# Cross-attention and quantised feed-forward on one core: a text group's last values added straight from PSUM, the x1 fill spread over the units, weight maxima run beside ScalarE's background

## The chip, the cores and the metric

One core of one Trainium2 chip runs the whole program. The time is device microseconds of that core, from the program's start to its end; several runs of a kernel give a median, and one further run is recorded by the hardware profiler. Engines are named as the profile names them: PE (TensorE, with PEld for its weight loads), DVE (VectorE), ACT (ScalarE), POOL (GpSimd) and SP (SyncE, which only issues DMAs here).

## The reference, cut to what matters

```python
# x (4, 1024, 512), ctx (4, 1024, 512); 16 heads of 32
q = layernorm(x) @ Wq + bq ; k = ctx @ Wk + bk ; v = ctx @ Wv + bv
# mask per batch: 768 image tokens attend within their own chunk of 256;
# 256 text tokens attend to all image tokens and causally to text
x1  = x + softmax(q k^T / sqrt(32) where mask) v @ Wo + bo
xq  = fake_quant(layernorm(x1))          # one scale: the maximum over the whole tensor
h   = fake_quant(silu(xq @ wg_q^T) * (xq @ wu_q^T))   # again one scale for all of it
out = x1 + h @ wd_q^T                    # wg_q, wu_q, wd_q: int8-rounded, a scale per row
```

The two scales over whole tensors cut the program into three stages that follow each other: attention up to x1, gate and up products, down product.

## The kernel before, in words

**Tiling of the attention.** The 4096 tokens are cut into 16 chunks of 256 (`B * NQB`); of the four chunks of a batch three are image and the last is text. A `Block` is one chunk of queries, and a group is four heads of it (four groups). An image group has one part, since it sees only its own chunk of keys; a text group has four parts, one for each chunk of keys (part 3 is the causal diagonal). A `Unit` is a block, a group and a part: 112 units in all, 12 image units and then 16 text units for each of the first three batches; the last batch runs one image block (4 units), the text block (16) and two image blocks (8).

**The loop.** `for n in range(len(units) + V_LAG)` (L821) works on three units at a time. Iteration n does, in this order: `weights` of unit n-5 (scores transposed into PSUM with the row maximum subtracted, L488 and L492 on PE, exponential on ACT, L494); `maxima` of unit n (scores L442 on PE, then on DVE four row maxima, L445 for image and L449 for text, with the mask added first, L448, where a text part is odd); the sums over keys of unit n-5 on POOL (L514); `minus_maxima` after a group's last part (POOL L465 and L466, and in the next iteration a transposing DMA, L473, whose tile `nmT` the `weights` of that group's part 0 read); the x1 fill (L848 to L855); a background item; `values` of unit n-6 (L532 on PE, 4 heads side by side); ACT's copy of the result (L881); one large step of projections or of the output product (`large`, all at L225 on PE); the second background item; and so on. The four engines PE, DVE, ACT and POOL run in exactly the order in which the code issues their work (`manual_schedule`, L777); SP's queue is not in that list, and its order is chosen when the program is built.

**PSUM.** All tiles of the attention stage come from one pool of 8 banks, each 128 x 512 f32. A bank is used again as soon as its readers are done. The bank `av` of `values` (L522) has two halves of 256 columns: half 0 takes the values (L532), half 1 takes the sums of the exponentials over the keys (L555, matmuls with a block of ones), which are made only for a group's last part.

**A text group's sum over its parts.** Part 0 is copied to `oT` by ACT (L543); parts 1 and 2 are added to `oT` by DVE straight from PSUM (L545). The last part is not added there: after the sums have come in, ACT copies both halves to SBUF (`avs`, L881), and in the next iteration `quotient` (L566) takes the reciprocal of the sums on DVE (L567), adds `oT` to the values in SBUF on DVE (L569, text only) and multiplies on POOL (L570).

**From unit 84 on** (`LATE`, L658) the large steps are halved, so that iterations are shorter there.

**x1 in DRAM.** x1 begins as the output bias (a DMA from SP, L853) plus x (an accumulating DMA that POOL issues, L855), chunk by chunk; later `Output.load` reads a chunk (L584), the output product is added (L588), moments are taken (L595 to L598), and POOL's queue writes it back (L601).

**The background.** A queue holds the layer norm's steps (`statistics` on DVE, `deviation` and `apply` on ACT and POOL), the moments of x1 (DVE) and, from iteration 49 on, the 22 tiles of the gate and up weights: `largest` (DVE L636 to L638), `quantise` (ACT L641, POOL L642), and a transposing DMA (L646). An iteration takes one item; if that was `quantise`, it takes the next one too.

**After the attention.** L1055 is the gate and up product, L1146 and L1158 the down product. The change does not touch them.

Of the kernel before, what the change touches and what calls it, by code (L numbers as in the profile page):

```python
# [14 lines left out]
ALU = mybir.AluOpType  # L15
# [5 lines left out]
B, N, C = 4, 1024, 512  # L21
# [5 lines left out]
NQB = N // QB  # L27
# [15 lines left out]
def kernel(ctx: ExitStack, tc: tile.TileContext, x, kv, Wq, bq, Wk, bk, Wv, bv, Wo, bo, clip_x, clip_down, w_gate, w_up, w_down, out):  # L43
    nc = tc.nc
# [77 lines left out]
    with ExitStack() as actx:  # L122
# [9 lines left out]
        def bank(name):  # L132
            return ps_b.tile([P, 512], F32, tag="b", name=name)
# [212 lines left out]
        background = deque()  # L346
# [54 lines left out]
        def rows_of(j):  # L401
            return slice(j * D, (j + 1) * D)
# [115 lines left out]
        def values(u):  # L518


            k, g = u.k, u.g
            av = bank(f"av_{u.n}").rearrange("p (a q) -> p a q", a=2)  # L522
            if u.part == 0 and g == 0:
                k.begin()
            o = k.oT[:, g, :]
            diag = k.text and u.part == TEXT
            last = u.part == u.parts - 1
            va = V[k.keys[u.part]]
            for n in range(2):
                cols = slice(P, QB) if diag and n else slice(0, QB)  # L530
                for j in range(4):
                    nc.tensor.matmul(  # L532
                        av[rows_of(j), 0, cols],
                        va[:, n, g * P + j * D : g * P + (j + 1) * D],
                        u.pT[:, j, n, cols],
                        start=(n == 0),
                        stop=(n == 1),
                        tile_position=(0, j * D),
                        skip_group_check=True,
                    )  # L540
            if not last:
                if u.part == 0:
                    nc.scalar.copy(o, av[:, 0, :])  # L543
                else:
                    nc.vector.tensor_tensor(o, av[:, 0, :], o, ALU.add)  # L545
            if last:
                terms = []
                if ("sum", k.n, g) in state:
                    terms.append((state.pop(("sum", k.n, g)), slice(0, QB)))
                if u.direct:  # L550
                    terms += [(u.pT[:, :, n, :], slice(P, QB) if diag and n else slice(0, QB)) for n in range(2)]
                for n, (sp, cols) in enumerate(terms):
                    for j in range(4):

                        nc.tensor.matmul(  # L555
                            av[rows_of(j), 1, cols],
                            ones[:, :D],
                            sp[:, j, cols],
                            start=False,
                            stop=(n == len(terms) - 1),  # L560
                            tile_position=(0, j * D),
                            skip_group_check=True,
                        )
                avs = small.tile([P, 2, QB], F32, tag="avs", name=f"avs_{u.n}", bufs=2)

                def quotient():  # L566
                    nc.vector.reciprocal(avs[:, 1, :], avs[:, 1, :])  # L567
                    if k.text:
                        nc.vector.tensor_tensor(avs[:, 0, :], avs[:, 0, :], o, ALU.add)  # L569
                    nc.gpsimd.tensor_tensor(o, avs[:, 0, :], avs[:, 1, :], ALU.mult)  # L570

                return avs, av, quotient

# [77 lines left out]
        units = []  # L651
        for b in range(B):
            for qb in range(NQB) if b < B - 1 else (0, TEXT, 1, 2):
                k = Block(b, qb)
# [68 lines left out]
        def need_rows(kind, c, g, n):  # L723

            while rows_done.get((kind, c), 0) <= g:
                advance(n)

        def need_values(c, n):
            while ("v", c) not in done:
                advance(n)  # L730
# [56 lines left out]
                nc.tensor.matmul(tail.pos[i], tail.k.oT[:, cc, i * P : (i + 1) * P], W["Wo"][:, cc, :], start=False, stop=(cc == NCC - 1))  # L787

        weight_stages, n_weights = deque(), 0
        last_small = None  # L790

        def send(a):
# [28 lines left out]
        for n in range(len(units) + V_LAG):  # L821
            previous = units[n - 1] if 0 < n <= len(units) else None
            if n < len(units):
                u = units[n]
                half = u.part % 2
                for c in u.k.keys[2 * half : 2 * half + 2] if u.k.text else u.k.keys:
                    need_rows("k", c, u.g, n)
                need_rows("q", u.k.c, u.g, n)

            def shifts_of_previous():  # L830
                if previous is not None and previous.part == previous.parts - 1:
                    shifts(previous)

            if T_LAG <= n < len(units) + T_LAG:
                sums = weights(units[n - T_LAG], shifts_of_previous)
            else:
                shifts_of_previous()
                sums = None
            if n < len(units):
                maxima(u)  # L840
            if sums is not None:
                sums()
            if n < len(units) and u.part == u.parts - 1:
                minus_maxima(u)
            if n in (2, 3, 4, 5):
                (spread, sigmoids, product, total)[n - 2]()

            for first, c in ((True, (n - 5) // 3), (False, (n - 7) // 3)):  # L848
                rows = slice(c * QB, (c + 1) * QB)
                if not 0 <= c < B * NQB or (n - (5 if first else 7)) % 3:  # L850
                    continue
                if first:
                    nc.sync.dma_start(x1_d[rows, :].rearrange("(t p) c -> p t c", p=P), bo_b.unsqueeze(1).to_broadcast([P, QB // P, C]))  # L853
                else:
                    nc.gpsimd.dma_start(x1_d[rows, :], x_tok[rows, :], accum_op=ALU.add, max_dma_last_dim=C)  # L855
            t = units[n - T_LAG] if T_LAG <= n < LATE else None
            crowded = t is not None and t.k.text and t.part > 1
            while sum(b.__name__ == "moments" for b in background) > 1:
                background.popleft()()
            f = background.popleft() if background and n > 0 and not (crowded and background[0].__name__ == "deviation") else None  # L860
            if f is not None and f.__name__ in ("deviation", "apply", "quantise"):
                f()
                f = background.popleft() if background and f.__name__ == "quantise" else None
            fs = list(later)
            later.clear()
            for g in fs:
                g()
            ends = None
            if n >= V_LAG:
                v = units[n - V_LAG]  # L870
                need_values(v.k.keys[v.part], n)
                if v.part == 0 and v.g == 0:
                    while len(outputs) + len(whole) >= OUTS:
                        step_output()
                if v is units[-5]:
                    tail.load()
                ends = values(v)
            if ends is not None:
                avs, av, quotient = ends
                if n < len(units) + V_LAG - 1:  # L880
                    nc.scalar.copy(avs, av)  # L881
            large(n)
            while whole:
                finished(whole.pop(0))
            if f is not None:
                f()
            if ends is not None and n < len(units) + V_LAG - 1:
                later.append(quotient)
            if n == len(units) + V_LAG - 2:
                assert not outputs  # L890
                tail_products(0, (0, 1))

            if weight_stages and quantised[0]:
                weight_stages.popleft()()
            if can_small(n):
                small_step()
            prepare_next(n)
            if n > n_img and n_weights < 2 * NIC and not weight_stages and len(background) < 2:
                stages = weight_unit(n_weights)
                background.extend(stages[:2])  # L900
                weight_stages.append(stages[2])
                n_weights += 1
            if n < LATE and spent + BIG < target(n) and can_big(n + 1):
                big_step()
            if n >= V_LAG:
                u = units[n - V_LAG]
                if u.part == u.parts - 1 and u.g == NCC - 1 and u is not units[-1]:
                    whole.append(u.k)
# [74 lines left out]
    with gctx:  # L983
# [83 lines left out]
        for tb in range(NTB):  # L1067
# [5 lines left out]
            for ic in range(NIC):  # L1073
                last = tb == NTB - 1 and ic >= NIC - 2
# [64 lines left out]
    for n, tb in enumerate(order):  # L1139
# [9 lines left out]
        o = out_tok[tb * TB : (tb + 1) * TB, :].rearrange("(t p) c -> p t c", p=P)  # L1149
# [65 lines left out]
```

## Time and profile before

| what | value |
|---|---|
| median of 3 runs | 1118.52 us (1116.16 to 1120.01) |
| the profiled execution's own time | 1117.18 us |
| its span in the profile | 1115.3 us |
| mean granted TensorE clock | 0.987 |
| busy: PE, DVE, POOL, ACT | 97%, 76%, 48%, 47% |
| attention | 0 to about 872 us |
| gate and up products | about 872 to 1032 us |
| down product | 1032 us to the end |
| text groups in the trace (iterations of their `values`) | about 180 to 287, 384 to 491, 588 to 690, 716 to 809 us |

"Busy" counts the time in which an engine has at least one instruction in work. An idle stretch of an engine is listed with what ended it. The granted clock is the share of TensorE's full clock that its throttle lets through. The chain of waits runs back from the last instruction, at each step to what released it. Times within the trace count from the span's start.

### The profile page before, as it was taken

What the parts mean: (1) busy time and instruction counts of PE and PEld (TensorE: products, weight loads), DVE (VectorE), ACT (ScalarE), POOL (GpSimd) and SP (SyncE); (2) the same over time, 40 slices, a digit from 0 to 9 for tenths busy, and PEclk for the clock granted to TensorE, in tenths of its full rate; (3) what the DMA queues carried; (4) which work ended last, traced back from release to release, by engine and by line L of the source; (5) the groups of instructions that cost most, each with busy time, mean ns of one, the idle gap of its engine ahead of it and who ended that gap; (6) DMA issues with size and microseconds to landing.
All of it is one profiled execution on the core that took longest, in us unless ns stands there. A gap on an engine that the chain in (4) does not pass through costs nothing.

```text
span 1115.3 us, 32159 instructions
## 1 busy us (share of the span) xinstructions
PE 1087.0 (97%) x13851; PEld 585.9 (53%) x13851; DVE 846.9 (76%) x1316; ACT 522.1 (47%) x941; POOL 531.0 (48%) x615
## 2 busy tenths in 40 slices
PE   9998999999999999999999999989999899998998
PEld 5555555465655555565545556655554344443444
DVE  2555678797688959778786887987777788877887
ACT  3344444354445435454533455554443565553653
POOL 1224447678764567775446666765642221110110
PEclk9998999999999999999999999998999899999999
DMA  7369636355645454332222122212211698311895
GB/s 236 93 202 284 144 80 133 72 117 102 121 63 115 94 117 85 108 82 65 92 73 67 42 77 61 60 53 80 72 66 58 203 287 247 75 34 39 300 382 193
DMA packets 138262, 135.91 MB, mean 122 GB/s; under 512 B 56060, under 2 KB 103432, under 8 KB 136712
## 3 DMA queue, kind: packets, MB, share of 16 engines
q1 hardware_dynamic: 115600, 91.91, 29.6%
q0 software_dynamic: 22208, 41.42, 14.1%
q8 instruction: 108, 1.77, 0.7%
q10 hardware_dynamic: 312, 0.53, 0.2%
q14 instruction: 34, 0.28, 0.1%
HBM read 79.96 MB, written 50.07 MB: 117 GB/s over the span
## 4 chain that ended last, share of the span: by engine, by line
PE 81%; DMA 6%; DVE 5%; POOL 3%; issue 2%; ACT 2%; SPq 1%; DVEq 0%; POOLq 0%; ACTq 0%
PE po L225 9%; PE av L532 8%; PE pv L225 8%; PE pp_q L225 8%; PE pp_kv L225 8%; PE s L442 8%; PE t L492 7%; PE pg L1055 7%; PE pu L1055 7%; PE t L488 3%; PE av L555 3%; PE pd L1158 2%; POOL sp L514 2%; DMA xt<-x_d 2%; ACT pT L494 1%
## 5 line engine op out<-in xcount | busy, mean ns | idle before, releaser
L494 ACT ACTIVATE pT<-t 128x512 f32<-128x512 f32 x448 | 231.3, 603 | 135.7 <-PE t L492 135.5
L514 POOL TENSOR_TENSOR sp<-pT 128x1024 f32<-128x1024 f32 x59 | 140.8, 2386 | 173.8 <-ACT pT L494 173.7
L514 POOL TENSOR_TENSOR sp<-sp,pT 128x1024 f32<-128x1024 f32 x84 | 188.8, 2248 | 46.8 <-ACT pT L494 43.5
L449 DVE TENSOR_REDUCE nmh<-s 128x1 f32<-128x512 f32 (+1 forms) x256 | 159.2, 655 | 46.7 <-PE s L442 42.3
L445 DVE TENSOR_REDUCE nmh<-s 128x2 f32<-128x512 f32 x192 | 119.0, 683 | 58.9 <-PE s L442 58.9
L442 PE MATMUL s<-kT,qT 32*128 32x256 f32 (+1 forms) x1792 | 128.5, 376 | 3.1 <-DVE xr L588 2.5
L532 PE MATMUL av<-pT,va 128*32 128x256 f32 (+1 forms) x1792 | 118.9, 383 | 1.7 <-ACT pT L494 1.4
L225 PE MATMUL pp_q<-qT,Wq_sb 128*32 128x256 f32 x2048 | 117.4, 379 | 0.0
L225 PE MATMUL pv<-Wv_sb,kvT 128*32 128x512 f32 (+1 forms) x1088 | 116.3, 567 | 0.0
L492 PE MATMUL t<-qT,kT 32*128 32x256 f32 (+1 forms) x1792 | 115.1, 371 | 0.0
L225 PE MATMUL po<-Wo_sb,oT 128*32 128x512 f32 (+1 forms) x1120 | 110.9, 536 | 0.0
L567 DVE RECIPROCAL avs<-avs 128x256 f32<-128x256 f32 x63 | 109.9, 1744 | 0.0
L225 PE MATMUL pp_kv<-kvT,Wk_sb 128*32 128x256 f32 x1920 | 109.0, 379 | 0.0
L442 PEld LDWEIGHTS s<-kT,qT 32*128 32x128 f32 x1792 | 99.0, 187 | 16.1 <-DVE xr L588 3.4
L492 PEld LDWEIGHTS t<-qT,kT 32*128 32x128 f32 x1792 | 89.6, 186 | 7.2 <-issue 0.7
L1055 PE MATMUL pg<-xqT,wgT 128*128 128x512 bf16 x352 | 91.0, 382 | 0.5 <-DVE xqT L1016 0.5
L225 PEld LDWEIGHTS pp_q<-qT,Wq_sb 128*32 128x32 f32 x2048 | 67.7, 110 | 44.9 <-issue 3.6
L1055 PE MATMUL pu<-xqT,wuT 128*128 128x512 bf16 x352 | 90.6, 381 | 0.0
L1061 ACT ACTIVATE silu<-pg,sg 128x512 f32<-128x512 f32 x88 | 60.0, 686 | 64.9 <-PE pg L1055 64.9
L1082 DVE SCALAR_TENSOR_TENSOR h<-pu,su,silu 128x512 f32<-128x512 f32 x88 | 65.4, 747 | 30.2 <-PE pu L1055 29.2
L225 PEld LDWEIGHTS pp_kv<-kvT,Wk_sb 128*32 128x32 f32 x1920 | 63.8, 110 | 42.7 <-issue 4.5
L532 PEld LDWEIGHTS av<-pT,va 128*32 128x32 f32 x1792 | 48.6, 110 | 56.7 <-ACT pT L494 27.2
(190 smaller groups left out, 1340.5 us busy)
## 6 DMA issues: line engine op xcount, KB each, us to landing
xt<-x_d SPq DMA_DIRECT2D x16, 1024.0 KB, 6.4
h<-h_d POOLq DMA_DIRECT2D x3, 2816.0 KB, 13.7
xb<-in_x_dram SPq DMA_DIRECT2D x16, 512.0 KB, 4.3
x_d<-bo_b SPq DMA_DIRECT2D x16, 512.0 KB, 7.0
x_d<-in_x_dram POOLq DMA_DIRECT2D x16, 512.0 KB, 6.8
xr<-x_d SPq DMA_DIRECT2D x16, 512.0 KB, 3.7
x_d<-xr POOLq DMA_DIRECT2D x16, 512.0 KB, 3.3
spread_kv<-in_ctx_dram SPq DMA_DIRECT2D x60, 128.0 KB, 3.0
```

Of the source, the lines that this page charges most:

```text
L225: nc.tensor.matmul(out[rows_of(j)], lhs[:, rows_of(j)], rhs, start=start, stop=stop, tile_position=(0, j * D), skip_group_check=True)
L442: nc.tensor.matmul(s[j][:, m * QB : m * QB + w], q[rows_of(j), g, rows], key[rows_of(j), g, :w], start=True, stop=True)
L445: nc.vector.tensor_reduce(nmh[:, j, :, 0], s[j].rearrange("p (i q) -> p i q", i=2), AX.X, ALU.max, negate=True)
L449: nc.vector.tensor_reduce(nmh[:, j, i, half : half + 1], s[j][:, :n], AX.X, ALU.max, negate=True)
L492: nc.tensor.matmul(t[j][:, n, cols], kc[rows_of(j), g, n * P : (n + 1) * P], q[rows_of(j), g, cols], start=False, stop=(n == 1))
L494: nc.scalar.activation(pT[:, j], t[j], AF.Exp)
L514: nc.gpsimd.tensor_tensor(sp[:, :, cols], a, pT[:, :, n, cols], ALU.add)
L532: nc.tensor.matmul(av[rows_of(j), 0, cols], va[:, n, g * P + j * D : g * P + (j + 1) * D], u.pT[:, j, n, cols], start=(n == 0), stop=(n == 1),
L567: nc.vector.reciprocal(avs[:, 1, :], avs[:, 1, :])
L1055: nc.tensor.matmul(ps, w[:, cc, ic * P : (ic + 1) * P], qT[:, cc, :], start=(cc == 0), stop=(cc == NCC - 1))
L1061: nc.scalar.activation(s, pg, AF.Silu, scale=sg[:, ic : ic + 1])
L1082: nc.vector.scalar_tensor_tensor(h[:, ic, :], pu, su[:, ic : ic + 1], s, ALU.mult, ALU.mult)
```

## The change

Three edits, in the diff below. `values`: the last part of a text group is now added to `oT` by DVE straight from PSUM too, directly after its L532 matmuls in the program's order and ahead of the sums' matmuls; ACT then copies only the sums' half; `quotient` loses its SBUF add, and POOL multiplies `oT` in place. The loop: the fill of chunk c is asked for two iterations after the last unit of its block instead of at iteration 5 + 3c, and the accumulating DMA two iterations later, as before; the last chunks are moved up to fit. The background: after `deviation`, `apply` or `quantise` an iteration also takes the next item when that is one of DVE's (`statistics`, `largest`, `moments`), and not otherwise.

```diff
@@ values
-            if not last:
-                if u.part == 0:
-                    nc.scalar.copy(o, av[:, 0, :])
-                else:
-                    nc.vector.tensor_tensor(o, av[:, 0, :], o, ALU.add)
+            if k.text and u.part == 0:
+                nc.scalar.copy(o, av[:, 0, :])
+            elif k.text:
+                nc.vector.tensor_tensor(o, av[:, 0, :], o, ALU.add)
             if last:
                 terms = []
...
                 def quotient():
                     nc.vector.reciprocal(avs[:, 1, :], avs[:, 1, :])
-                    if k.text:
-                        nc.vector.tensor_tensor(avs[:, 0, :], avs[:, 0, :], o, ALU.add)
-                    nc.gpsimd.tensor_tensor(o, avs[:, 0, :], avs[:, 1, :], ALU.mult)
+                    nc.gpsimd.tensor_tensor(o, o if k.text else avs[:, 0, :], avs[:, 1, :], ALU.mult)
@@ before the loop
+        fill_at = {}
+        for c in range(B * NQB):
+            at = min(max(n for n, u in enumerate(units) if u.k.c == c) + 2, len(units) - 6)
+            while at in fill_at:
+                at += 1
+            fill_at[at] = c
@@ in the loop
-            for first, c in ((True, (n - 5) // 3), (False, (n - 7) // 3)):
+            for first, c in ((True, fill_at.get(n)), (False, fill_at.get(n - 2))):
+                if c is None:
+                    continue
                 rows = slice(c * QB, (c + 1) * QB)
-                if not 0 <= c < B * NQB or (n - (5 if first else 7)) % 3:
-                    continue
                 if first:
...
             if f is not None and f.__name__ in ("deviation", "apply", "quantise"):
                 f()
-                f = background.popleft() if background and f.__name__ == "quantise" else None
+                f = background.popleft() if background and background[0].__name__ in ("statistics", "largest", "moments") else None
...
                 avs, av, quotient = ends
                 if n < len(units) + V_LAG - 1:
-                    nc.scalar.copy(avs, av)
+                    nc.scalar.copy(avs[:, 1:] if v.k.text else avs, av[:, 1:] if v.k.text else av)
```

In the changed kernel the add stands at L544, the sums' matmuls at L554, the reciprocal at L566, POOL's multiply at L567 and ACT's copy at L884.

## The prediction

> **What bounds the kernel now.** I read the page first: busy times, then the slices, then the chain of waits.
>
> ```profile
> PE 1087.0 (97%) x13851; PEld 585.9 (53%) x13851; DVE 846.9 (76%) x1316; ACT 522.1 (47%) x941; POOL 531.0 (48%) x615
> ...
> PE   9998999999999999999999999989999899998998
> ...
> PEclk9998999999999999999999999998999899999999
> ```
>
> PE is busy 97% of the span, and the digits show no slice of the attention below 8. By the timeline of PE, it idles some 0.5 us in all between 120 and 640 us. So a wait of PE there is paid in full, and work taken off DVE (76%) is worth only what PE waits for it. PE's waits lie mainly after 650 us, where iterations are shorter (about 5 us against 6.5 to 7). The next view is DVE's groups by form, for what the first edit removes and adds:
>
> ```profile
> L569 DVE TENSOR_TENSOR avs<-avs,oT 128x256 f32<-128x256 f32 x16 | 28.9, 1809 | 0.0
> ...
> L545 DVE TENSOR_TENSOR oT<-av,oT 128x256 f32<-128x256 f32 x32 | 13.4, 419 | 0.2 <-PE av L532 0.2
> ```
>
> **Part 1, the values. What it removes:** 16 adds of 1.809 us, 28.9 us of DVE. It adds 16 like L545 at 0.419, 6.7 us. ACT's copy loses half its columns; ACT is 47% busy and the add ends long before the copy's other input, so 0.
>
> **What it adds: a wait of PE on DVE.** Before, a last part ran L532 (values) and L555 (sums) back to back into the two halves of one bank. Now DVE reads the first half between them. In the program as built, in all 16 text groups, the first sums matmul carries a wait on DVE whose count is exactly that of the new add; before, that matmul waited for POOL only. On DVE the add stands, in all 16, directly behind the iteration's four row maxima. So PE's order is values, wait, sums, and DVE's order is maxima, add. A group in the PE and then the DVE timeline:
>
> ```profile
> 205.24 0.86 PE L532 MATMUL av<-pT,va 128*32 128x256 f32 x16 [0.17 <-ACT pT L494]
> 205.89 0.64 PE L555 MATMUL av<-sp,ones 128*32 128x256 f32 x8
> 206.32 3.64 PE L225 MATMUL po<-Wo_sb,oT 128*32 128x512 f32 x32
> ```
> ```profile
> 205.14 0.30 DVE L448 TENSOR_TENSOR s<-s,mask 128x128 f32<-128x128 f32 x1 [2.66 <-PE s L442]
> ...
> 207.87 0.56 DVE L449 TENSOR_REDUCE nmh<-s 128x1 f32<-128x384 f32 x1
> 210.02 0.69 DVE L588 TENSOR_TENSOR xr<-po,xr 128x512 f32<-128x512 f32 x1 [1.59 <-PE po L225]
> ```
>
> PE starts its sums at 205.89, but DVE ends its maxima at 207.87 + 0.56 = 208.43. With the add (0.42) PE may go on at 208.85: a stall of 2.96 us. Behind the waiting matmul on PE stand the rest of the sums, the large step L225, then the next iteration's t (L488, L492) and s (L442); for these wait ACT's exponentials, DVE's maxima and L588. Nothing else can fill PE. DVE had sat idle 2.66 us for s before these maxima, so taking L569 from DVE doesn't start them sooner; in all 16 groups DVE waits for s in this way.
>
> The same sum (end of maxima + 0.42 - start of L555) for each group: nine with masked maxima (205.89, 233.13, 409.70, 436.94, 613.52, 640.77, 689.22, 734.37, 757.80) give 2.95 to 3.04, together 26.7; seven with the unmasked ones of a following image block (259.50, 286.43, 463.31, 490.25, 666.61, 783.47, 808.14) give 2.30 to 2.62, together 16.6. **Sum +43.3 us.** Bounds: 0 if PE need not wait (first rival), 43.3 as it stands.
>
> **What the relief of DVE gives.** These are the places where PE waits, or an s group is stretched, because DVE is late behind L569 and its reciprocal:
> - s at 223.75, 427.57 and 631.39 stretched by 1.2 each, at 277.39, 481.20 and 680.17 by 0.87 each: 6.2.
> - 746.9 to 751: PE waits for banks behind L567 at 741.84, L569 at 743.50 (2.46) and weight maxima. That goes, but next late is the chain POOL sum, nm, nmT, which by its rows lets t start at 754.2 in place of 755.05: 0.85 gained of 3.3.
> - 770.3 to 780.7: t at 780.71 against its nmT, landed at 777.6: 3.1, slower clock included.
> - 792.5: s waits for a bank that L588 frees, behind L567 and L569 (lines below): 2.2, and 1.7 for the slow clock that follows. 817.4: 0.8.
>
> **Sum -14.9 us** (5.3 of it before LATE). The waits at 660.5, 725 and 728 come from POOL and stay. Bounds 0 to 14.9.
>
> ```profile
> 790.97 1.74 DVE L567 RECIPROCAL avs<-avs 128x256 f32<-128x256 f32 x1
> 792.63 2.37 DVE L569 TENSOR_TENSOR avs<-avs,oT 128x256 f32<-128x256 f32 x1
> 794.92 0.41 DVE L588 TENSOR_TENSOR xr<-po,xr 128x256 f32<-128x256 f32 x1
> ```
>
> **What a stall does to the clock.** Granted clock changes on a grid of 3.41 us, so I read windows on that grid (start:end, length, PE busy, PEld, DVE, ACT, POOL, then the clock):
>
> ```profile
> 728.12:731.53 3.41, 2.11 (x44) 1.12 (x39) 3.41 (x4) 0.47 (x1) 1.61 (x5) 1.00 0.13 29
> 769.08:772.49 3.41, 2.18 (x34) 0.87 (x27) 3.26 (x9) 1.08 (x2) 3.05 (x3) 1.00 0.08 11
> 772.49:779.31 6.82, 6.82 (x61) 4.40 (x64) 5.00 (x10) 2.06 (x4) 5.00 (x9) 0.50 0.67 218
> 792.97:796.38 3.41, 0.99 (x10) 0.68 (x10) 3.38 (x5) 1.64 (x4) 3.33 (x5) 1.00 0.00 0
> 796.38:799.79 3.41, 3.41 (x33) 1.58 (x36) 3.41 (x7) 0.00 (x0) 3.33 (x2) 0.50 0.10 19
> ```
>
> A window with 2.42 us of idle PE (792.97) is followed by one at half clock. So are the windows at 100.07, 864.65 and 1028.49 (busy 0.13, 1.53, 1.32), those with 1.2 to 1.5 idle once in three times (769.08; not 728.12, nor 1025.07 with 1.89 busy). Taking the limit at 1.7 idle, a stall S laid on the grid at random puts that much into one window with the chance (S + 0.01) / 3.41: for S = 2.96 this is 0.87, for 2.33 0.69; 9 x 0.87 + 7 x 0.69 = 12.7 drops. One window at half clock costs a PE-bound stretch 1.7 us; three of the five drops last two windows or more. I take 12 drops of one window, **+20 us**; bounds 0 and 16 x 2.7 = 43 (1.6 windows each).
>
> Two rules of the Trainium skill speak here. "PSUM — Partial Sum Buffer", section "PSUM bank collisions raise a hardware error", says that semaphores should guard PSUM by bank and quadrant and not by address; by address add and sums touch different columns and this change would have no wait (1104), by the bank it has one (the forecast). No run so far shows it; the waits built into the program follow the bank. "TensorE: Matmul & The Clock Gate", section "HAM oscillation — how this bites in real kernels", gives the rule "no PE-idle gaps >~3.4µs"; by it none of these stalls costs clock (1147), by the row at 792.97, a gap of 2.50 us, most of them do, and the row decides.
>
> **Part 2, the fill.** In the program as built the 16 fills L853 keep their early place on SP (trace: 73.9 to 106.4 us); only POOL's 16 accumulating DMAs move, from 88.7 to 434.8 us to iterations between 7 and 109. POOL spends 1.35 us on issuing one. Gain: none taken (PE idles 0.5 us where they leave, the bound; the 3.5 us wait at 103.7 is for DVE's maxima and stays). Loss: five come into LATE, behind that iteration's nm on POOL and ahead of its sums; if each came before a sum that PE waits for, 5 x 1.35 = 6.8. POOL is 48% busy, which hides them; I take 0.
>
> **Part 3, the background.** The same 22 x 0.98 us (0.67 + 0.15 + 0.16) of weight maxima move on DVE by about an iteration. DVE's idle time ahead of its maxima hides them (1.3 to 2.7 us in the rows above); where it doesn't, four fall into LATE: bounds -4 to +4, taken 0.
>
> **Sum on the profiled run:** 1117.2 + 43.3 - 14.9 + 20 = 1165.6. It is 1.3 below the median of the runs, so **1167**.
>
> **Rivals.**
> - *Faster: PE doesn't wait*, since the add comes before PE gets there. Then only the relief counts: 1118.5 - 14.9 = 1104. Against it: DVE is 2.3 to 3.0 us behind in all 16 rows. It decides if the stalls average under 14.9 / 16 = 0.93 us.
> - *Same, about 1118*: stalls of some 0.9 us, or a slack in PE that I don't see. Against it: 0.5 us of idle PE in 520 us.
> - *Stalls without clock*: 1118.5 + 43.3 - 14.9 = 1147.
> - *Worse*: two-window drops at every stall and no relief, POOL and DVE late in LATE: 1118.5 + 43.3 + 43 = 1205; half of that excess over the forecast, 1186.
> - *The fill part doesn't do what it says* (fills stay early): it changes no sum above.
>
> **How the numbers follow.** Stalls with some clock drops (1150 to 1185): 0.65; without drops (1140 to 1150): 0.14; worse (over 1185): 0.12; the same: 0.03; faster: 0.06. The range 1140 to 1192 takes in the first two and the nearer half of the worse case. Faster by over 0.3% (3.4 us, about what a measurement of this kernel can tell from no change) 0.06, within 0.3% 0.03, slower 0.91.
>
> **What would show it.** After: the sums matmul L554 with idle before it, released by DVE's add L544, 16 times, 2.3 to 3.0 us each, 43 in all; granted clock below 0.98, with windows of 0.50 behind some of these stalls between 200 and 640 us, where there are none now; no 2.4 us add on DVE, and no wait for L588 near 792. The forecast is wrong if L554 waits under a microsecond, if the clock stays whole (1147), or if POOL's issues hold up PE's sums after 660 us.

## The result, and the profile after

The changed kernel takes 1181.29 us (median of 5 runs, 1179.41 to 1184.63) against 1118.52: 1.0565 times as long, 95% interval 1.0541 to 1.059, or 62.8 us more. The profiled execution has a span of 1177.6 us, 62.3 more than before. The page's busy line and two rows of its slices, to be held against those of before:

```profile
PE 1099.8 (93%) x13829; PEld 586.0 (50%) x13851; DVE 823.1 (70%) x1316; ACT 519.2 (44%) x941; POOL 530.0 (45%) x615
...
PE   9998999999999988959999888888899899999898
...
PEclk9999999999999999979999899998999899999899
```

DVE has lost 23.8 us, as the first edit meant to. PE's idle time has risen from 28.3 us (1115.3 - 1087.0) to 77.8 (1177.6 - 1099.8), that is by 49.5, and its busy time by 12.8 with the same matmuls in the program (the trace has 22 records fewer): they ran at a lower clock (mean 0.969 against 0.987). The two make up the 62.3. In the view of waits of the changed kernel (time in all, times, longest) there is a line that did not exist before:

```profile
PE av L554 <- DVE oT L544: 47.2, 15, 11.8
```

It counts 15 of the 16 groups. In the sixteenth, at 484.69, POOL's sum L514 ended at 487.24, some 0.04 us after the add, and the view puts its 1.79 us of idle PE down to POOL.

One text group in the timelines of PE and of DVE, the same that the prediction showed:

```profile
203.95 0.86 PE L532 MATMUL av<-pT,va 128*32 128x256 f32 x16 [0.17 <-ACT pT L494]
207.61 1.08 PE L554 MATMUL av<-sp,ones 128*32 128x256 f32 x8 [2.80 <-DVE oT L544]
208.44 4.52 PE L225 MATMUL po<-Wo_sb,oT 128*32 128x512 f32 x32
```
```profile
206.58 0.56 DVE L449 TENSOR_REDUCE nmh<-s 128x1 f32<-128x384 f32 x1
207.05 0.41 DVE L544 TENSOR_TENSOR oT<-av,oT 128x256 f32<-128x256 f32 x1
```

The sums L554 start 3.66 us after the values L532, where before it was 0.65 (205.24 to 205.89). DVE ends the last of its four maxima at 207.14, adds until 207.46, and only then does PE go on. The large step behind it takes 4.52 us in place of 3.64. The windows on the clock's grid say why (start:end, length, PE busy, PEld, DVE, ACT, POOL, granted clock):

```profile
203.40:206.81 3.41, 1.24 (x28) 0.69 (x20) 2.82 (x8) 1.88 (x4) 1.45 (x1) 1.00 0.00 0
206.81:210.22 3.41, 2.61 (x20) 0.98 (x24) 0.66 (x2) 0.37 (x1) 0.89 (x1) 0.50 0.00 0
```

PE was busy for 1.24 us of the first window, and the next one has half clock.

One wait is much longer than the others: 11.83 us, in the group that before was at 490.25 (forecast 2.37). On PE:

```profile
513.00 0.86 PE L532 MATMUL av<-pT,va 128*32 128x256 f32 x16
525.69 1.08 PE L554 MATMUL av<-sp,ones 128*32 128x256 f32 x8 [11.83 <-DVE oT L544]
```

and on DVE in the same time:

```profile
508.76 0.41 DVE L544 TENSOR_TENSOR oT<-av,oT 128x256 f32<-128x256 f32 x1
519.13 0.69 DVE L359 BATCH_NORM_STATS2 st<-xb 128x6 f32<-128x512 f32 x1 [9.96 <-DMA xb<-in_x_dram]
...
522.77 2.44 DVE L445 TENSOR_REDUCE nmh<-s 128x2 f32<-128x512 f32 x4
525.13 0.41 DVE L544 TENSOR_TENSOR oT<-av,oT 128x256 f32<-128x256 f32 x1
```

DVE stood for 9.96 us at the statistics of a layer norm, whose block of x SP had asked for only at 511.94 and which landed at 519.1. Behind it on DVE stood the maxima and the add, and behind the add PE.

### The profile page after: what moved, and what is told of

Its sections match the earlier page's. It is cut to its first block, busy times and chain, and to the rows that moved or that the text cites. A ratio compares the mean times of both kernels' runs of the same rounds, so it can differ in the third digit from the quotient of the medians.

```text
span 1177.6 us, 32174 instructions
## 1 busy us (share of the span) xinstructions
PE 1099.8 (93%) x13829; PEld 586.0 (50%) x13851; DVE 823.1 (70%) x1316; ACT 519.2 (44%) x941; POOL 530.0 (45%) x615
## 3 DMA queue, kind: packets, MB, share of 16 engines
q8 instruction: 109, 1.79, 0.6%
## 4 chain that ended last, share of the span: by engine, by line
PE 76%; DMA 7%; DVE 6%; POOL 4%; ACT 3%; issue 3%; SPq 1%; DVEq 0%; POOLq 0%; ACTq 0%
PE pv L225 9%; PE po L225 8%; PE pp_q L225 8%; PE pp_kv L225 8%; PE t L492 7%; PE pg L1058 7%; PE pu L1058 6%; PE av L532 6%; PE s L442 6%; POOL sp L514 3%; PE av L554 3%; PE t L488 3%; PE pd L1161 2%; ACT pT L494 2%; DMA xt<-x_d 2%
## 5 line engine op out<-in xcount | busy, mean ns | idle before, releaser
L514 POOL TENSOR_TENSOR sp<-sp,pT 128x1024 f32<-128x1024 f32 x84 | 189.1, 2252 | 105.0 <-ACT pT L494 101.7
L514 POOL TENSOR_TENSOR sp<-pT 128x1024 f32<-128x1024 f32 x59 | 140.7, 2385 | 180.5 <-ACT pT L494 173.7
L442 PE MATMUL s<-kT,qT 32*128 32x256 f32 (+1 forms) x1792 | 123.2, 373 | 0.2 <-DVE xr L585 0.2
L225 PE MATMUL pp_q<-qT,Wq_sb 128*32 128x256 f32 x2048 | 121.8, 389 | 0.0
L532 PE MATMUL av<-pT,va 128*32 128x256 f32 (+1 forms) x1792 | 117.2, 379 | 1.9 <-ACT pT L494 1.2
L225 PE MATMUL pp_kv<-kvT,Wk_sb 128*32 128x256 f32 x1920 | 114.6, 393 | 0.0
L566 DVE RECIPROCAL avs<-avs 128x256 f32<-128x256 f32 x63 | 109.7, 1742 | 0.0
L442 PEld LDWEIGHTS s<-kT,qT 32*128 32x128 f32 x1792 | 96.2, 186 | 11.0 <-issue 1.2
L225 PEld LDWEIGHTS pp_kv<-kvT,Wk_sb 128*32 128x32 f32 x1920 | 66.2, 114 | 46.2 <-issue 9.2
L554 PE MATMUL av<-sp,ones 128*32 128x256 f32 x472 | 40.2, 415 | 49.0 <-DVE oT L544 47.2
```

The costliest lines, as they stand in the source:

```text
L225: nc.tensor.matmul(out[rows_of(j)], lhs[:, rows_of(j)], rhs, start=start, stop=stop, tile_position=(0, j * D), skip_group_check=True)
L442: nc.tensor.matmul(s[j][:, m * QB : m * QB + w], q[rows_of(j), g, rows], key[rows_of(j), g, :w], start=True, stop=True)
L514: nc.gpsimd.tensor_tensor(sp[:, :, cols], a, pT[:, :, n, cols], ALU.add)
L532: nc.tensor.matmul(av[rows_of(j), 0, cols], va[:, n, g * P + j * D : g * P + (j + 1) * D], u.pT[:, j, n, cols], start=(n == 0), stop=(n == 1),
L554: nc.tensor.matmul(av[rows_of(j), 1, cols], ones[:, :D], sp[:, j, cols], start=False, stop=(n == len(terms) - 1), tile_position=(0, j * D) ...
```

## The experiments

The first four take the change apart. Times are medians, beside runs of the kernel before on the same chip: 1119.38 for this set.

### The values edit alone

```diff
+ values edit (all three of its places)
  fill and background as before
```

> The values edit alone. Theory (PE's wait for the add is the cost): 16 waits at the sums' matmuls of 2.3 to 3.0 us, 43 in all, with most of them followed by a window of half clock; by the prediction's own sum 1118.5 + 43.3 - 14.9 + 20 = 1167. Rival (the 14 us by which the changed kernel was slower than forecast also come from the wait): 1181, as the whole change. Second rival (the wait is not the cost): under 1125.

1172.91 us, 1.0472 times the kernel before (1.045 to 1.0494). From the start of the last L532 matmul to the sums' start, less the 0.065 that back-to-back matmuls take there, the 16 groups lose 43.1 us; the forecast's sum was 43.3. The time lies between the theory's 1167 and its first rival's 1181, and the second rival, under 1125, is out. The waits view has all 16:

```profile
PE av L554 <- DVE oT L544: 39.7, 16, 2.8
```

(39.7 is idle time; the rest of the 43.1 is the tail of the values' matmuls, which drains in the wait.)

### The fill edit alone

```diff
+ fill_at, and the loop over it
  values and background as before
```

> The fill edit alone. Theory: SP asks for the fills at 73 to 106 us as before, only POOL's 16 accumulating DMAs move: 1118.5 within 2. Rival (POOL's DMA issues, 1.4 us each, hold up POOL's sums or the maxima's chain after 500 us): 1122 to 1126, with PE idle behind POOL near 508, 734 or 864.

1126.86 us, 1.0062 (1.0044 to 1.008): slower by 7.5, against the theory and as much as the rival allowed (1126 from 1118.5), but at the largest place not by the rival's mechanism. SP did ask for the fills at their early place. The place where PE loses most is near 697 (of the 10.5 us that this profiled execution is behind at the end of the attention, 8.7 arise there), and there SP's queue and DVE read:

```profile
690.57 0.36 SPq L137 DMA_DIRECT2D xr<-x_d  x1
691.04 2.98 SPq L147 DMA_DIRECT2D spread_q<-xn_d  x4
694.06 1.19 SPq L646 DMA_TRANSPOSE wuT<-wq_u  x1
695.35 0.52 SPq L633 DMA_DIRECT2D w_g<-in_L_ffn_w_gate_dram  x1
```
```profile
698.39 0.69 DVE L636 TENSOR_REDUCE sg<-w_g 128x1 f32<-128x512 f32 x1 [7.29 <-DMA w_g<-in_L_ffn_w_gate_dram]
```

The accumulating DMA left POOL at 683.8 and took 6.7 us to land, so x1 was in DRAM at about 690.5. SP's load of that chunk (`xr`, L137) went out at 690.57: it reads what the DMA writes. Behind it in SP's queue stood a weight load, asked for at 689.66 before and at 695.35 here. DVE waited 7.29 us for it (0.97 before), and PE 3.0 for DVE.

### The background edit alone

```diff
-                f = background.popleft() if background and f.__name__ == "quantise" else None
+                f = background.popleft() if background and background[0].__name__ in ("statistics", "largest", "moments") else None
```

> The background edit alone. In the changed kernel's trace one wait was 11.8 us instead of the 2.4 forecast: DVE stood at a layer norm's statistics, which the edit takes up an iteration earlier, for a block of x still loading (landed at 519). Theory (a rival to the forecast's nothing): the wait exists without the values edit too, but PE has its sums and a large step to do meanwhile, so PE loses 3 to 6: 1121 to 1125. If the wait is harmless alone: 1118.5 within 2. If it costs what it did in the changed kernel: 1128.

1120.41 us, 1.0014 (0.9994 to 1.0035): no difference that this comparison shows, so below the theory's 1121 to 1125. The wait does exist (DVE idle 6.65 us for the block of x, landed at 490.7), and PE loses 4.3 us in that iteration, but other places give most of it back: at the end of the attention the profiled execution is 1.4 us behind.

The expectation had the reason the wrong way round: the edit takes these statistics up later than the kernel before, not earlier. What is late is the load. The two rows of the kernel before, then those of this run:

```profile
449.24 0.39 SPq L137 DMA_DIRECT2D xb<-in_x_dram  x1
481.75 0.70 DVE L359 BATCH_NORM_STATS2 st<-xb 128x6 f32<-128x512 f32 x1
```
```profile
486.58 0.45 SPq L137 DMA_DIRECT2D xb<-in_x_dram  x1
490.68 0.69 DVE L359 BATCH_NORM_STATS2 st<-xb 128x6 f32<-128x512 f32 x1 [6.65 <-DMA xb<-in_x_dram]
```

Before, the block was asked for 32.5 us ahead of its use, here 4.1. The program asks for a block of x only when `apply` of the block before is done, and that `apply` (ACT L377) came at 477.13 here and at 444.24 before. The delay goes back to a `deviation` (ACT L364) at 435.00 here and 383.73 before: with the edit the items of the background come in another order.

### Fill and background without the values edit

```diff
+ fill edit, background edit
  values as before
```

> Fill and background together, no values edit. Theory: the sum of the two alone, 1118 to 1125, so that the values edit accounts for at least 55 of the 63 us. Rival (the parts cost by meeting each other): over 1130.

1128.44 us, 1.0071 (1.0046 to 1.0096): 9.1 above the kernel before, near the two alone together (7.5 + 1.0), but above the theory's 1118 to 1125 and below the rival's 1130. At the iteration of the long wait, though, PE loses 8.4 us, not the 4.3 of the background alone: POOL's accumulating DMA of that chunk leaves at 483.8, while the block of x is asked for at 487.8, and the load takes 7.1 us where it took 4.1 without the fill.

The next four ask about the mechanisms; the kernel before took 1117.15 us beside them.

### The add after the sums

```diff
-            elif k.text:
+            elif k.text and not last:
                 nc.vector.tensor_tensor(o, av[:, 0, :], o, ALU.add)
...
+                if k.text:
+                    nc.vector.tensor_tensor(o, av[:, 0, :], o, ALU.add)
                 avs = small.tile(...)
```

> The values edit alone, but with the last part's add asked for after the sums' matmuls instead of ahead of them: the add is the same, only who waits for whom is turned round. Theory (the wait of PE is the whole cost): PE runs values and sums back to back again, no idle before the sums, and DVE is relieved as forecast, by 14.9 at most and, from what the values-only run showed late in the attention, by some 8: 1104 to 1112. Rival (the PSUM read itself, or the lost SBUF copy, is what costs): about 1173.

1105.86 us, 0.9907 (0.9872 to 0.9942). The same add, the same bank, the same DVE time; only its place behind the sums differs, and that is worth 67 us against the values edit alone (65 when each is held against the kernel before of its own set). On PE:

```profile
202.96 0.86 PE L532 MATMUL av<-pT,va 128*32 128x256 f32 x16 [0.17 <-ACT pT L494]
203.61 0.64 PE L554 MATMUL av<-sp,ones 128*32 128x256 f32 x8
```

Values and sums run back to back again. The add starts at 206.06 on DVE, behind the maxima as in the change, and PE no longer waits for it. Now it is ACT's copy of the sums that waits for the add, 29.1 us in all in the 16 groups; no wait of PE in this trace goes back to that copy.

### The sums in a bank of their own

```diff
+                av2 = bank(f"as_{u.n}").rearrange("p (a q) -> p a q", a=2) if k.text else av
-                            av[rows_of(j), 1, cols],
+                            av2[rows_of(j), 1, cols],
-                            start=False,
+                            start=k.text and n == 0,
...
-                return avs, av, quotient
+                return avs, av2, quotient
```

> The values edit alone, add ahead of the sums as in the change, but the sums go to a PSUM bank of their own. Theory (PE waits because add and sums share a bank): no wait of the sums for the add; a ninth claim on the 8 banks may make others wait, 1105 to 1125. Rival (PE waits for the add whatever the bank, by its order in the program): 1173.

1109.22 us, 0.992 (0.9897 to 0.9942). The add is ahead of the sums in the program as in the change, and none of the 16 groups waits for it. So it is the shared bank that makes the wait. (The run gives the sums a bank and a tile of their own at once; which of the two the program's wait goes by, it does not tell apart.) The further claim on the banks costs nothing that can be told from the run above.

### The values three times

```diff
-            for n in range(2):
+            for n in (0, 1) * (3 if k.text and last else 1):
```

> The values edit alone, with the values' matmuls of each text group's last part done three times into the same place (same result, 1.3 to 1.7 us more work of PE inside a wait of 2.3 to 3.0). The waits end when they did, since DVE's maxima set them; only PE is idle for about 1 us instead of nearly 3. Theory (the stalls cost their length and, besides, half clock in the windows after them): half-clock windows behind the stalls vanish, 19 us less than the values-only run's 1173, so 1154. Rival (half clock after a stall is hidden anyway): 1173 or more.

1150.5 us, 1.0289 (1.0268 to 1.0311): 22.4 less than the values edit alone, with more work on PE. The same group:

```profile
203.88 2.16 PE L532 MATMUL av<-pT,va 128*32 128x256 f32 x48 [0.17 <-ACT pT L494]
207.54 0.64 PE L554 MATMUL av<-sp,ones 128*32 128x256 f32 x8 [1.50 <-DVE oT L544]
```
```profile
204.27:207.68 3.41, 1.91 (x51) 1.39 (x44) 3.02 (x8) 0.93 (x2) 2.34 (x1) 1.00 0.00 0
207.68:211.10 3.42, 3.42 (x40) 1.27 (x35) 0.00 (x0) 0.37 (x1) 0.00 (x0) 1.00 0.02 5
```

The same group in the values edit alone, on that run's grid:

```profile
206.91:210.32 3.41, 0.60 (x16) 0.44 (x16) 2.64 (x8) 0.54 (x2) 2.33 (x1) 1.00 0.00 0
210.32:213.74 3.42, 3.42 (x24) 1.09 (x20) 0.00 (x0) 0.37 (x1) 0.00 (x0) 0.50 0.02 5
```

From values to sums it still takes 3.66 us, but PE is busy for 1.91 us of the window in place of 0.60, and the next window keeps its clock. The mean clock rises from 0.972 to 0.991. Time lost to the clock is (1 - 0.972) x 1170.8 = 32.8 us without, (1 - 0.991) x 1148.3 = 10.3 with: 22.5 less, as much as the time fell. Not all of it lies behind the waits: between 200 us and the end of the attention the values edit alone has 14 windows at half clock and this run 2, which at 1.7 us each makes 20.5; the rest are drops near 104 us and at the very end.

### The fill six iterations sooner

```diff
-            at = min(max(...) + 2, len(units) - 6)
+            at = max(5, min(max(...) + 2, len(units) - 6) - 6)
```

> The fill edit alone, with every chunk asked for six iterations sooner than in the change. In the fill-only run SP's load of a block of x1 stood waiting for the accumulating DMA to land near 690, and behind it on SP a weight load, for which DVE and then PE waited 3 us. Theory (SP's queue behind that load costs the 7 us): 1118.5 within 2. Rival (POOL's DMA issues so late in the attention cost them): 1124 to 1128 still.

1123.24 us, 1.0057 (1.0032 to 1.0082), which the interval does not tell apart from the fill edit as it was (1.0062). (One of the five runs took 2832.92 us; the interval leaves it out, and the other four lie between 1120.14 and 1125.9.) The theory's 1118.5 is missed; the rival's range began at 1124. The trace shows half of it: DVE's wait for the weight load falls from 7.29 us to 1.3, and PE's stretch at 697 is gone. But at 776.07 an accumulating DMA of 1.29 us now stands on POOL ahead of a weight's cast; the weight's transposing DMA leaves SP 2 us later than before (778.01 against 776.00), nmT stands behind it, and PE waits 3.65 us for nmT at 784.19. At the end of the attention this profiled execution is 3.5 us behind, the fill edit's was 10.5. How the 7.5 us divide between SP's queue and POOL's issues stays open.

The last four put things together; the kernel before took 1118.52 us beside them.

### The whole change, without statistics as a second item

```diff
-                f = background.popleft() if background and background[0].__name__ in ("statistics", "largest", "moments") else None
+                f = background.popleft() if background and background[0].__name__ in ("largest", "moments") else None
```

> The whole change, except that the background's second item may not be a layer norm's statistics (only weight maxima and moments). Theory (DVE's statistics, taken up an iteration early while their block of x is still loading, made one of the 16 waits 11.8 us long): that wait falls back to 2.4 or so, and the time by 6 to 10: 1171 to 1176. Rival (the load is late whatever asks for it, or something else holds PE there): 1181.

1183.38 us, 1.0599 (1.0562 to 1.0636): my theory that this gives back 6 to 10 us falls. The long wait for statistics went, but there are two others, 9.5 and about 9 us of PE. In the timeline of DVE and of PE:

```profile
299.88 1.99 DVE L260 STREAM_TRANSPOSE qT<-spread_q 128x1024 f32<-128x1024 f32 x1 [9.32 <-DMA spread_q<-xn_d]
```
```profile
304.71 1.08 PE L554 MATMUL av<-sp,ones 128*32 128x256 f32 x8 [9.47 <-DVE oT L544]
```

This run does not give the statistics their old place back: in the kernel before they could follow `quantise`, here they can only be an iteration's first item. The block behind the first of these waits has its statistics at 264.2 us, where they stood at 230.7 in the changed kernel and at 230.6 before, four iterations later than in either. So the normalised block is written later too, and its load comes after DVE has got to it. In both versions DVE waits for a load ahead of the maxima and the add; with the add's wait, PE pays nearly all of that. A run that adds DVE's items and leaves the order of the others as it was is missing.

### The whole change, with the add after the sums

```diff
+ the late add, in the changed kernel
```

> The whole change with the last part's add after the sums' matmuls. Theory (costs add up: late add 11 to 13 below the kernel before, fill 7 to 8 above, background 0 to 4 above): 1112 to 1120. Rival (the fill's and the background's waits hide in the stalls and come out when these go): 1120 to 1126.

1117.36 us, 0.999 (0.997 to 1.001): no different from the kernel before, and inside the theory's range. Fill and background take back 9.8 (against the late add again, below) of the 11 us that the late add gives.

### The late add with the background, without statistics and fill

```diff
+ the late add; background's second item "largest" or "moments" only
  fill as before
```

> Late add and the background edit without statistics, no fill edit: the parts that cost nothing by the runs so far. Theory (background moves weight maxima by an iteration, and DVE's idle time hides it): the late add's own time within 3, 1103 to 1108. Rival (maxima next to ScalarE's item relieve DVE late in the attention): 1098 to 1103.

1115.89 us, 0.9974 (0.9961 to 0.9987): a miss for both theories, some 8 slower than the late add alone. It has the wait for spread_q of the run before last (DVE idle 9.78 us until 287.90). Here PE does its sums and a large step meanwhile and then idles 2.5 us; that iteration is 6.5 us longer.

### The late add again

```diff
+ the late add alone, as above
```

> The late add alone once more, beside the run before on the same chip, for the interval: 1104 to 1108; one of its four times was 1112.6.

1107.52 us, 0.9905 (0.9888 to 0.9922). This is the fastest kernel of all: 1% below the kernel before, and it needs neither the fill nor the background edit.

## Why the prediction was right, and where its sum was off

The mechanism held: PE waits at the sums for an add that stands behind four maxima on DVE, because both use one bank. Turning the order round (late add) or parting the banks takes the wait away, and nothing else of the edit changes. The time, 1181, lies in the range and 14 above the forecast of 1167. Term by term:

| term | forecast | measured | from |
|---|---|---|---|
| 16 waits of PE | +43.3 | +43.1 | values edit alone, its timeline |
| half clock behind them | +20 | +22.4 | values thrice against values alone |
| relief of DVE | -14.9 | -11.0 | the late add again (1107.52 - 1118.52) |
| fill and background | 0 | +8.4 | whole change against values alone (1181.29 - 1172.91) |

The first three measured terms give 1118.5 + 43.1 + 22.4 - 11.0 = 1173.0, and the values edit alone took 1172.9. With the fourth it is the 1181.3 of the whole change. That this closes to 0.1 us is luck, since the terms come from sets whose own kernels before took 1117.15 to 1119.38. With each run held against its own, the clock's term is 20.2 and the fourth 9.2, and 43.1 + 20.2 - 11.0 = 52.3 stands against the 53.5 of the values edit alone.

- *The waits* were right group by group: 15 of the 16 in the changed kernel lie within 0.3 us of the forecast (each taken from L532's start to the sums' start, less the 0.65 of before). The sixteenth, 11.8 for 2.4, belongs to the fourth term.
- *The clock* was right in size and kind. I took 12 drops; in the values-alone trace 12 windows of PE after 200 us and before 880 are followed by half clock, 11 of them at one of the 16 waits and one at a wait for nmT. In the rows, stalls of less than 3 us were enough (206.91 of the values edit alone: 0.60 us busy, the next window at half clock). The Trainium skill's "TensorE: Matmul & The Clock Gate", section "HAM oscillation — how this bites in real kernels", with its gaps of 3.4 us, would have had none of these 11: no wait of that kernel's sums is longer than 2.8 us. The runs decide for the row that the prediction went by.
- *The bank*: what the Trainium skill's "PSUM — Partial Sum Buffer", section "PSUM bank collisions raise a hardware error", says of guarding by bank and not by address fits how this program is built. What that costs, the run with a bank of its own shows: 1109.22 in place of 1172.91.
- *The relief* was over-sized by 3.9, and by more if only the attention counts: at its end the late add's second trace is 8.7 us ahead of the kernel before, and the rest comes after it, where the edit changes nothing and the kernel before happens to have a drop of the clock (868.06) that the other has not. Before LATE it came nearly as forecast, 4.7 for 5.3 (the stretched s groups are gone in both late-add traces). In LATE the t at 780.7 was misread: I had its nmT land at 777.6 and took 3.1, but the trace has that nmT asked for by SP at 777.24 and landed at 779.65, 1.1 ahead of t. With DVE early PE just reaches nmT sooner and waits 3.19 us for it (at 770.44 in the first late-add trace), since nmT stands on SP behind a weight's transposing DMA and that behind POOL's cast, as before.
- *Fill and background at nothing* was the term that failed. For the fill I named POOL's issues as the only cost and bounded them at 6.8. The measured 7.5 is near that bound, but the trace shows another way: SP's load of a chunk waits until the fill has landed, and a weight load stands behind it. I had looked at what the fill's instructions cost, and not at who reads what they write. For the background I counted weight maxima and missed that the edit changes the order of the layer norm's items too: `apply` of one block slips (502.11 in the changed kernel, 444.24 before), the next block of x is asked for only behind it (511.94, before 449.24), and DVE stands at its statistics until 519.13. The load took 7.2 us there, beside the moved accumulating DMA of 507.95, and 4.1 in the run without the fill edit. DVE's wait for a load was not among my bounds. Held unit by unit against the values edit alone, the changed kernel's trace goes from 4.8 us ahead to 5.8 behind at this one wait and is 6.1 behind at the end of the attention. So the term of 8 to 9 us lies there; that the slipped `apply` and the slower load make it is read from these rows, and no run puts the order back and keeps the rest.
- *The rivals*: faster (1104) and same (1118) are out, since the waits are as long as the rows said; without clock (1147) is what the values-thrice run comes to, 1150.5, by taking the clock's part away. That the fills stay early on SP (73.3 to 106.1 us after) was right, but "it changes no sum" was not.
- *The 0.5 us of idle PE* between 120 and 640 us, by which the prediction argued against its rivals, are 1.3 in the trace (busy 518.66 of 520.00). No term goes by it.

## What to carry to other kernels

When two engines use one PSUM bank, as here, the order in which the program names them decides who waits: a read between two groups of matmuls tied TensorE to whatever stood ahead of that read on VectorE, and the same read behind the last matmul cost TensorE nothing. Before pricing such an edit, lay the two engines' timelines beside each other and measure how late the reader is; on a TensorE that is busy 97% that lateness was the price, and the clock added half as much again. For a transfer that is moved, ask who reads what it writes, and what stands behind that reader in its queue. For items of a queue that change places, ask which loads wait for each of them.

## What the runs showed of the hardware that was not expected

A stall shorter than a window of the grid is enough to lose the clock, and the limit is nearly sharp. In the 14 traces of this case, between 110 us and the end of the attention, I took each window of 3.41 us at whole clock by how long PE was busy in it, on each run's own grid, and looked at the window behind it:

| PE busy in the window, us | windows | followed by half clock |
|---|---|---|
| up to 1.36 | 44 | 44 |
| 1.38 to 1.70 | 16 | 6 |
| 1.70 to 2.00 | 23 | 0 |
| 2.00 to 2.70 | 63 | 4 |
| over 2.70 | 2912 | 0 |

So 2.05 us of idle PE in one window always cost the clock here, and 1.71 or less nearly never did. The four exceptions are the window at 769.08 of the kernel before (2.18 busy), one at the same place of the fill asked for sooner (768.85) and two of the fill edit alone (755.31 and 782.61, 2.09 and 2.60 busy); I have no explanation for them. Where the attention passes into the next stage the limit is looser: windows with 1.95 us busy (871.25 of the fill asked for sooner, 878.19 of the fill edit alone) are followed by half clock too. A stall of 3 us that the grid cuts in the middle costs no clock: the stall behind the values at 422.92 of the changed kernel left 1.75 and 2.11 us busy in its two windows (421.86 and 425.27), and both that follow run at 1.00.
